# Score maxima as 768-column tiles in three banks, four views of one shared tile, and layer-1 experts by 128 places plus four experts' last 32

## The chip, the cores and the metric

One core of a Trainium2 chip runs the whole program in one launch. The metric is the device time of one execution in microseconds (us). A kernel's time here is the median of several executions; a profile is of one further execution, with a record of each instruction on each engine.

## The reference

Four sequences of 1024 tokens with 128 channels pass through two layers. Each layer has attention and then a mixture of eight experts, both with an adaptive layer norm in front and a gate behind.

```python
# layer 0: causal attention with one head, then top-2 of 8 experts, GELU, no limit on an expert's places
# layer 1, attention: 16 heads of 8 channels, not causal
scores = einsum("bhqd,bhkd->bhqk", q, k) / sqrt(8); attn = softmax(scores); ctx = attn @ v
# ... plus a second attention (rank 64) that keeps the largest 204 of 1024 weights of each row,
# both mixed by sigmoid(lam), then a norm, a feed-forward (128 -> 512 -> 128, ReLU) and a norm
# layer 1, experts: top-2 of 8, each expert takes at most int(1024 / 8 * 1.25) = 160 places per sequence
h = relu(buf @ W1[e] + b1[e]); y = h @ W2[e] + b2[e]        # buf: (expert, sequence, 160, 128)
```

Everything is float32. A softmax may subtract any number from its row that keeps the exponentials in range; the kernel subtracts the row's maximum.

## The kernel before

The program is written with pools of tiles, and its instructions are issued in the order in which Python runs (`manual_schedule`). The tile layer adds the semaphore waits. Work that may run beside the main loop is written as generators. `Part` wraps one, and a small planner (`spend`, `grouped`, `outlook`, `worth`) keeps a clock for each engine and decides after every half step which Part's next piece is put there. That sets the order on all engines.

PSUM has eight banks of 512 f32 columns. Before, they are shared out as two tiles of two banks (`psb`, tag "big"), three tiles of one bank (`ps`, tag "ms", the shared banks) and one bank (`psa`) for attention outputs.

The main loop is layer 1's 16-head attention. A unit is one sequence, one group of four heads and one half of the queries (512): 32 units. It has two interleaved streams.

- *Maxima* (`maxima`, L1622 and L1626) of the unit ahead. For 128 queries and 512 keys, two heads at a time, `pm` gets two matmuls with 32 contraction rows each, on two row groups of TensorE. VectorE reduces the 1024 columns to two maxima. 16 such tiles make a unit. `shifted` turns the maxima into an extra row of the queries (`qa`), so that scores come out already shifted.
- *Weighed scores* (`weighed`, L1638 and L1642). For 128 keys and 512 queries, one matmul `pw` per head into a shared bank, and ScalarE's exponential into `prT`. `values` (L1660) then multiplies by V into `pav`.

A half step of the loop is two `weighed` (two heads), one step of `maxima` on the two other row groups, and four `values` matmuls of the step before. There are 512 half steps; 20 steps of the maxima come earlier, in `prologue`.

Beside the loop run: `begin` (norm and projections of the next sequence), `looked` (the rank-64 attention with a search for its 204 largest weights: `pk` L1393, its maximum L1398, its exponential L1401, transposes `ptk` L1420, output `po` L1425), `end` (output projection, feed-forward `ph` L1726 and `pf` L1739) and `sends` (routing, and scattering of tokens to the experts' places in DRAM). All but `pk` take shared banks; `pk` takes a "big" tile.

After the loop comes layer 1's expert stage, `worked_on(1, ...)`. Each expert's 160 places of a sequence are loaded as two tiles of 80, transposed (L829), modulated (L886), multiplied up (`ph` L839 into a "big" tile, ReLU L844), down (`py` L854, 80 rows each), given the bias (L859), and each tile's rows are scattered to the tokens' rows by GpSimd (L864). `taken_in` adds the two results of a token. Layer 0's experts use the same function with tiles of 128 places.

Of the kernel before, what the change touches and what calls it, by code (L numbers as in the profile page):

```python
# [9 lines left out]
F32 = mybir.dt.float32  # L10
# [17 lines left out]
RUNS = (((0, 3), (3, 2)), ((0, 2),))  # L28
DEEP = (P, CAP // 2)
# [12 lines left out]
GROUPS, SOON, EARLY_P, EARLY, AHEAD = 3, 0.5, -0.3, -0.1, 0.03  # L42
LOST, LATE = 0.2, 0.5
TAX_A, TAX_D = (0.4, 3), (1.5, 2)
LAST = (18, 20, 30, -3, 33, 7, 60, 38, 50, 54)
ROWS = ["out_b", "vp_b", "ff2_b", "ln1_g", "ln1_b", "ln2_g", "ln2_b"]


@with_exitstack
def kernel(ctx: ExitStack, tc: tile.TileContext, a: dict, out: bass.AP):  # L50
# [10 lines left out]
    psb = order.enter_context(tc.tile_pool(name="big", bufs=2, space=PSUM))  # L61
    ps = order.enter_context(tc.tile_pool(name="ps", bufs=3, space=PSUM))
    psa = order.enter_context(tc.tile_pool(name="av", bufs=1, space=PSUM))

# [29 lines left out]
    row = {n: rows[:, k, :] for k, n in enumerate(ROWS)}  # L94
    router = [load(f"router{l}", [P, E], a[f"router{l}"]) for l in range(2)]
# [79 lines left out]
    o_b = load("o_b", [P, C], a["o_w"][DH : DH + 1, 0, :].to_broadcast([P, C]))  # L175
# [50 lines left out]
    def more_constants():  # L226

        nc.vector.tensor_reduce(
# [4 lines left out]
        nc.vector.tensor_scalar_mul(o_b, o_b, sig)  # L233
# [96 lines left out]
    wide = [0.0, 0.0]  # L330
    costs = {}
# [21 lines left out]
    def grouped(free=free, banks=banks, wide=wide):  # L353

        free["P"] = max(free["P"], banks[1], wide[0]) + 1.05
        del wide[0]
        wide.append(spend(("D", 1.22), free=free))
        for _ in range(2):
            del banks[0]
            banks.append(spend(("A", 0.6), free=free))  # L360

    def outlook(ops=(), ready=0.0):

        f, b, w = dict(free), list(banks), list(wide)
        spend(*ops, after=ready, shared=True, free=f, banks=b)
        for _ in range(GROUPS):
            grouped(f, b, w)
            f["P"] += 0.55
        return f["P"]
# [4 lines left out]
    class Part:  # L374
# [37 lines left out]
        def go(self):  # L412
# [11 lines left out]
            costs[self.pieces.__name__, self.done] = ops  # L424
            self.ready = spend(*ops, after=self.ready, shared=True)
            if "!" in self.wants:
                self.ready = 0.0
# [97 lines left out]
    def routed(l, b, hT, wgt, wgtT, pool, ps, places=None, hs=(0, 1)):  # L525
# [18 lines left out]
        yield "D", ("P", 0.21 * n)  # L544
# [9 lines left out]
        yield "D", ("D", 1.0), ("A", 0.3)  # L554
# [27 lines left out]
        if l == 1 or places is not None:  # L582
# [15 lines left out]
            yield "D", ("P", 0.4)  # L598
# [5 lines left out]
        if places is not None:  # L604
# [9 lines left out]
            yield "D", ("D", 1.5)  # L614
# [193 lines left out]
    def worked_on(l, q, w1, w2, b2r, act, fp, then=None):  # L808

        n, p = PLACES[l], DEEP[l]  # L810
        units = [(e, i0, m) for e in range(E) for i0, m in RUNS[l]]
        most = max(m for _, m in RUNS[l])
        gots, hss, hids, gos = {}, {}, {}, {}

        def at(u, t):
            e, i0, m = u
            return t[l][q][e * n + i0 * p : e * n + (i0 + m) * p].rearrange("(m p) c -> p m c", p=p)

        def load(u):
            m = u[2]  # L820
            gots[u] = fp.tile([P, most, C + l], F32, tag="got", bufs=4, name=f"got{l}{q}")
            got = nc.sync.dma_start(out=gots[u][:p, :m], in_=at(u, sent))
            behind(got, sent_by[l, q], "a place that any of them may have filled")

        def shift(u):
            m = u[2]
            pt = ps.tile([P, m, p], F32, tag="ms", name=f"ptg{l}{q}")
            for i in range(m):
                nc.tensor.transpose(pt[:, i, :], gots[u][:p, i, :C], ident[:p, :p])  # L829
            hss[u] = fp.tile([P, most * p], F32, tag="hs", name=f"hs{l}{q}")  # L830
            return pt, hss[u][:, : m * p]

        def up(u, k0):
            e, _, m = u
            if k0 == 0:
                hids[u] = fp.tile([P, NK, most * p], F32, tag="hid", name=f"hid{l}{q}")
            ph = psb.tile([P, 2, 512], F32, tag="big", name=f"ph{l}{q}")
            for k in range(k0, k0 + 2):
                nc.tensor.matmul(  # L839
                    ph[:, k - k0, : m * p], lhsT=w1[:, e, k * P : (k + 1) * P],  # L840
                    rhs=hss[u][:, : m * p], start=True, stop=True,
                )
            for k in range(k0, k0 + 2):
                nc.scalar.activation(  # L844
                    hids[u][:, k, : m * p], ph[:, k - k0, : m * p], act,
                    bias=b1[l][:, e * NK + k : e * NK + k + 1],
                )

        def down(u):
            e, _, m = u  # L850
            py = ps.tile([P, m, C], F32, tag="ms", name=f"py{l}{q}")
            for i in range(m):
                for k in range(NK):
                    nc.tensor.matmul(  # L854
                        py[:p, i, :], lhsT=hids[u][:, k, i * p : (i + 1) * p],
                        rhs=w2[:, e, k, :], start=(k == 0), stop=(k == NK - 1),
                    )
            y = fp.tile([P, most, C], F32, tag="y", name=f"y{l}{q}", bufs=3)
            nc.vector.tensor_tensor(y[:p, :m], py[:p], rows_of(b2r[:, e, :], m)[:p], ALU.add)  # L859
            if l == 0:  # L860
                nc.sync.dma_start(out=at(u, done), in_=y[:p, :m])
                return
            for i in range(m):
                to = nc.gpsimd.indirect_dma_start(  # L864
                    out=done[l][q][:],
                    out_offset=bass.IndirectOffsetOnAxis(ap=gos[u][:p, i : i + 1], axis=0),
                    in_=y[:p, i, :],
                    in_offset=None,
                    bounds_check=2 * T - 1,
                    oob_is_err=False,  # L870
                )
                tc.declare_no_dep(to.ins, group=f"done{l}{q}", reason="rows differ")
                tc.add_to_no_dep_group(f"done{l}{q}", to.ins)
                done_by.setdefault(q, []).append(to.ins)
# [4 lines left out]
        for i in range(len(units) + 2):  # L879
            if i < len(units):  # L880
                u = units[i]
                if i + 2 < len(units):
                    load(units[i + 2])
                pt, hs = shift(u)
                if l:
                    nc.vector.tensor_scalar(  # L886
                        hs, pt.rearrange("c m p -> c (m p)"), cols[1][:, 4, q : q + 1],
                        cols[1][:, 3, q : q + 1], ALU.mult, ALU.add,
                    )
                    gos[u] = fp.tile([P, most], mybir.dt.int32, tag="go", bufs=4, name=f"go{q}")  # L890
                    nc.vector.tensor_copy(gos[u][:p, : u[2]], gots[u][:p, : u[2], C])
                else:
                    nc.vector.tensor_copy(hs, pt.rearrange("c m p -> c (m p)"))
                yield "A!", ("P", 0.25 * u[2]), ("D", 0.15 + u[2] * p * 0.0011)
# [1114 lines left out]
```

## Time and profile before

| | us |
|---|---|
| median of 6 runs (lowest to highest) | 2047.17 (2035.39 to 2062.0) |
| the profiled execution | 2044.29 |
| its span, first to last instruction | 2042.4 |
| TensorE matmul (PE) busy | 1811.1 (89%) |
| VectorE (DVE) busy | 1285.7 (63%) |
| ScalarE (ACT) busy | 1144.8 (56%) |
| GpSimd (POOL) busy | 494.2 (24%) |
| mean granted TensorE clock | 0.933 |

PE is matmuls, PEld weight loads, which overlap matmuls. Matmuls are pipelined and their ends are modelled, so that a busy PE need not be at its peak. An f32 matmul shows as two records, one for each pass. In a line of groups: line, engine, operation, output and inputs, shapes, count, then busy us, mean ns of one, and the engine's idle time before them with what ended it. In a line of the timeline: start us, length us, engine, line, operation; in brackets the idle time before, and who ended it. "issue" is waiting that the profile does not explain. The granted clock is TensorE's, 1.00 being full speed.

### The profile page before, as it was taken

The page shows a single profiled execution, that of the slowest core. Times are in us where ns is not written, and L with a number is a line of the kernel's source. Part 1 is how long each engine was busy: PE and PEld are TensorE (multiplying, and loading weights), DVE is VectorE, ACT ScalarE, POOL GpSimd, SP SyncE. Part 2 cuts the span into 40 slices and gives each one's busy share as a digit, 9 for nine tenths or more (in the row PEclk, how much of TensorE's full clock was granted, in tenths as well). Part 3 has the DMA queues.
Part 4 walks back from the last instruction along what each step waited for, and adds up shares of the span by engine and source line. Part 5 has one row for each costly group of instructions (what it writes and reads, how often), then busy time and mean ns, then how long its engine had stood idle before and what let it go on. Part 6 is the DMA issues. An engine that isn't in the chain of part 4 may idle for free.

```text
span 2042.4 us, 33750 instructions
## 1 busy us (share of the span) xinstructions
PE 1811.1 (89%) x12805; PEld 928.1 (45%) x12805; DVE 1285.7 (63%) x3174; ACT 1144.8 (56%) x2317; POOL 494.2 (24%) x539
## 2 busy tenths in 40 slices
PE   6875888888899999998999999998998989997875
PEld 5654666552233434433343434334343424354875
DVE  4664413456788696577876666877666698842523
ACT  3442324225686755586864568785457876553432
POOL 1033345204111011103231111212211032321453
PEclk9997889898899999998998999999899999998987
DMA  8511223211000000000000000000000000003223
GB/s 283 163 42 39 63 66 87 65 34 29 19 1 27 6 2 7 1 6 6 22 18 3 6 1 6 6 22 19 4 5 5 5 9 10 8 1 114 68 69 85
DMA packets 82779, 73.11 MB, mean 36 GB/s; under 512 B 13327, under 2 KB 72035, under 8 KB 82608
## 3 DMA queue, kind: packets, MB, share of 16 engines
q1 hardware_dynamic: 73984, 56.93, 9.1%
q0 software_dynamic: 8192, 13.54, 2.3%
q8 instruction: 103, 1.69, 0.3%
q14 instruction: 68, 0.56, 0.1%
q10 hardware_dynamic: 432, 0.40, 0.1%
HBM read 35.79 MB, written 36.75 MB: 36 GB/s over the span
## 4 chain that ended last, share of the span: by engine, by line
PE 65%; DVE 12%; ACT 9%; issue 8%; POOL 2%; DMA 2%; another core or an unknown queue 1%; SPq 0%; POOLq 0%; ACTq 0%; DVEq 0%
PE pw L1638 26%; PE pav L1660 11%; PE py L854 4%; PE ph L839 4%; DVE mxh L1626 3%; PE po L1425 3%; PE pm L1622 2%; ACT prT L1642 2%; DVE nm L1398 2%; ACT junk L1492 2%; PE pf L1739 2%; ACT exq L1401 1%; PE ph L1726 1%; PE pk L1393 1%
## 5 line engine op out<-in xcount | busy, mean ns | idle before, releaser
L1626 DVE TENSOR_REDUCE mxh<-pm 128x2 f32<-128x1024 f32 x512 | 620.7, 1220 | 243.2 <-PE pm L1622 228.3
L1638 PE MATMUL pw<-qa,kg 32*128 32x512 f32 x2048 | 716.4, 660 | 56.7 <-ACT prT L1642 34.2
L1642 ACT ACTIVATE prT<-pw 128x512 f32<-128x512 f32 x1024 | 557.0, 596 | 339.6 <-PE pm L1622 199.7
L1622 PE MATMUL pm<-kg,qg 32*128 32x512 f32 x2048 | 602.6, 668 | 7.2 <-DMA qg<-qk 6.6
L1638 PEld LDWEIGHTS pw<-qa,kg 32*128 32x128 f32 x2048 | 220.2, 189 | 331.1 <-issue 160.2
L1660 PE MATMUL pav<-prT,v_more 128*9 128x256 f32 x3584 | 289.2, 395 | 0.0
L844 ACT ACTIVATE hid<-ph,b 128x160 f32<-128x160 f32 (+2 forms) x256 | 101.1, 457 | 230.3 <-PE ph L839 189.7
L1660 PEld LDWEIGHTS pav<-prT,v_more 128*9 128x9 f32 x3584 | 53.7, 89 | 356.7 <-issue 356.2
L1492 ACT ACTIVATE junk<-exq,now 128x1024 bf16<-128x1024 f32 x160 | 184.8, 1155 | 9.5 <-DVE now L1519 8.8
L1622 PEld LDWEIGHTS pm<-kg,qg 32*128 32x128 f32 x2048 | 162.2, 191 | 20.0 <-issue 8.9
L839 PE MATMUL ph<-hs,w 128*128 128x160 f32 (+2 forms) x512 | 138.2, 412 | 30.2 <-DVE hs L886 11.2
L1575 POOL TENSOR_TENSOR exq<-exq,lfq 128x512 f32<-128x512 f32 x64 | 80.9, 1286 | 343.8 <-DVE lfq L1573 336.2
L854 PE MATMUL py<-w,hid 128*128 128x128 f32 (+1 forms) x1152 | 146.1, 284 | 5.8 <-issue 5.1
L854 PEld LDWEIGHTS py<-w,hid 128*128 128x128 f32 (+1 forms) x1152 | 141.7, 181 | 12.9 <-issue 8.3
L839 PEld LDWEIGHTS ph<-hs,w 128*128 128x128 f32 x512 | 90.6, 210 | 60.2 <-issue 18.8
L859 DVE TENSOR_TENSOR y<-py,b2r 128x384 f32<-128x384 f32 (+1 forms) x64 | 29.1, 454 | 121.1 <-PE py L854 63.6
L917 POOL DMA_INDIRECT ys<-done,outof x64 | 64.2, 1003 | 167.9 <-DMA qg<-qk 68.9
L786 POOL DMA_INDIRECT sent<-xns,into x64 | 63.7, 995 | 91.9 <-DVE into L626 32.3
L864 POOL DMA_INDIRECT done<-y,go x64 | 59.6, 932 | 62.1 <-DVE y L859 17.0
L490 POOL TENSOR_TENSOR rs_l<-rs_l,mhalf 128x8 f32<-128x8 f32 (+1 forms) x10 | 14.0, 1401 | 246.3 <-DVE rs_l L489 246.3
L1425 PE MATMUL po<-sV,exT 128*128 128x129 f32 x512 | 67.4, 285 | 2.2 <-ACT exT L1421 1.1
L1425 PEld LDWEIGHTS po<-sV,exT 128*128 128x128 f32 x512 | 61.2, 195 | 16.5 <-ACT exT L1421 4.9
(532 smaller groups left out, 2221.2 us busy)
## 6 DMA issues: line engine op xcount, KB each, us to landing
w<-in_w_dram SPq DMA_DIRECT2D x32, 256.0 KB
sent<-zero SPq DMA_DIRECT2D x2, 2560.0 KB
done<-zero SPq DMA_DIRECT2D x4, 1024.0 KB
qk<-near SPq DMA_DIRECT2D x8, 512.0 KB
ys<-done SPq DMA_DIRECT2D x16, 256.0 KB
got<-sent SPq DMA_DIRECT2D x16, 192.0 KB
done<-y SPq DMA_DIRECT2D x16, 192.0 KB
sent<-nowhere SPq DMA_DIRECT2D x4, 645.0 KB
```

What stands on the lines that cost most here:

```text
L839: nc.tensor.matmul(ph[:, k - k0, : m * p], lhsT=w1[:, e, k * P : (k + 1) * P], rhs=hss[u][:, : m * p], start=True, stop=True,)
L844: nc.scalar.activation(hids[u][:, k, : m * p], ph[:, k - k0, : m * p], act, bias=b1[l][:, e * NK + k : e * NK + k + 1],)
L854: nc.tensor.matmul(py[:p, i, :], lhsT=hids[u][:, k, i * p : (i + 1) * p], rhs=w2[:, e, k, :], start=(k == 0), stop=(k == NK - 1),)
L917: nc.gpsimd.indirect_dma_start(out=y, out_offset=None, in_=done[0][b // 2][:], in_offset=bass.IndirectOffsetOnAxis(ap=outof[:, i, k : k + ...
L1425: nc.tensor.matmul(po, lhsT=exT[:, k, :], rhs=sVs[b % 2][:, k, :], start=(k == 0), stop=(k == NT - 1),)
L1492: nc.scalar.activation(junk, ex, AF.Sign, bias=now[:, i, 0:1], scale=-1.0, accum_out=now[:, i, 1:2],)
L1575: nc.gpsimd.tensor_tensor(ex[:, half(h)], ex[:, half(h)], lf[:, half(h)], ALU.subtract)
L1622: nc.tensor.matmul(pm[:, jj, :], lhsT=qg[js, t0 : t0 + P], rhs=kg[js, half(kh)], start=True, stop=True,)
L1626: nc.vector.tensor_reduce(mx[:, q, j0 : j0 + 2, kh], pm, AX.X, ALU.max)
L1638: nc.tensor.matmul(pw, lhsT=need(b, g, h)[1][js, k * P : (k + 1) * P], rhs=qas[b, g, h][js, :], start=True, stop=True,)
L1642: nc.scalar.activation(prs[b, g, h, k][:, j, :], pw, AF.Exp)
L1660: nc.tensor.matmul(to, lhsT=v, rhs=pr[:, j, cs], start=(k == 0), stop=((k, part) == (NT - 1, 1)),)
```

## The change

PSUM in the main loop is shared out anew. The three shared banks and the two "big" tiles are closed at its start. One tile of four banks, `ps4`, takes their place as four views that are handed out in turn (`Turns.split`), and one tile of three banks, `pm3`, holds the maxima. The score columns go to `pm3` in quarters of 256: three quarters make one reduce of 768 columns, first in `pm3`'s first half, then in its second. A matmul of 512 columns that would cross from one half to the other, or a bank's end, is split in two. `pk` takes two neighbouring views of `ps4`. After the loop `pm3` is closed, and three more shared tiles of one bank join the four views.

Layer 1's experts get a function of their own. An expert's first 128 places make one tile. The last 32 of four experts are loaded into one tile together; their down-projection writes four blocks of 32 output rows. Biases for these come in `b2l`.

Also: `o_b` is read into `rows` later and scaled in `prologue`; three yields of `routed` are merged into their successors; the planner knows the new tiles (`thirds`), the two-view request ("2") and other constants (`SOON` 0.5 to 0.3, `TAX_A` 3 to 2.25). In the loop the heads' order is exchanged between `weighed` and `maxima`.

```diff
+class Turns:
+    def __init__(self, pool, n):
+        self.turns = [pool.tile] * n
+    def tile(self, shape, dt, **kw):
+        self.turns.append(self.turns.pop(0))
+        return self.turns[-1](shape, dt, **kw)
+    def split(self, banks, n):
+        def of(i):
+            def view(shape, dt, **kw):
+                t = banks[: shape[0], i, : math.prod(shape[1:])]
+                return t if len(shape) == 2 else t.rearrange("p (a b) -> p a b", b=shape[2])
+            return view
+        self.banks, self.turns = banks, [of(i) for i in range(n)]
...
+    def two(self, skip):
+        if self.of[self.turns[0]] % 2:
+            self.turns.append(self.turns.pop(0))
+            skip()
+        i = self.of[self.turns[0]]
...
+        return self.banks[:, i : i + 2].rearrange("p a k -> p (a k)")
...
-    psb = order.enter_context(tc.tile_pool(name="big", bufs=2, space=PSUM))
-    ps = order.enter_context(tc.tile_pool(name="ps", bufs=3, space=PSUM))
     psa = order.enter_context(tc.tile_pool(name="av", bufs=1, space=PSUM))
+    ps_ctx = order.enter_context(ExitStack())
+    ps = Turns(ps_ctx.enter_context(tc.tile_pool(name="ps", bufs=3, space=PSUM)), 3)
+    psb = ps_ctx.enter_context(tc.tile_pool(name="big", bufs=2, space=PSUM))
...
             def looked_at(b, qt, ex, z):
-                pk = psb.tile([P, T], F32, tag="big", name="pk")
+                if general:
+                    pk = psb.tile([P, T], F32, tag="big", name="pk")
+                else:
+                    pk = ps.two(lambda: banks.append(banks.pop(0)))
...
             def maxima(b, g, h):
-                        for j0 in (2, 0):
-                            pm = psb.tile([P, 2, 512], F32, tag="big", name="pm")
+                        for j0 in (0, 2):
+                            if not three:
+                                pm = psb.tile([P, 2, 512], F32, tag="big", name="pm")
                             for jj in range(2):
                                 js = slice(32 * (j0 + jj), 32 * (j0 + jj) + 32)
+                                done_ = 0
+                                while done_ < 2:
+                                    m = 2 - done_
+                                    if three:
+                                        at = three_at[0] + len(quarters)
+                                        m = min(m, 3 - len(quarters), 2 - at % 2)
+                                        to = three[0][:, at : at + m].rearrange("p a k -> p (a k)")
...
+                                    nc.tensor.matmul(
+                                        to, lhsT=qg[js, t0 : t0 + P],
+                                        rhs=kg[js, k0 : k0 + 256 * m], start=True, stop=True,
+                                    )
...
+                                    if len(quarters) == 3 or (last_one and jj == 1 and done_ == 2 and quarters):
+                                        at, m = three_at[0], len(quarters)
+                                        nc.vector.tensor_reduce(
+                                            mx[:, quarters[0] : quarters[0] + m],
+                                            three[0][:, at : at + m], AX.X, ALU.max,
+                                        )
+                                        quarters.clear()
+                                        three_at[0] = 3 - at
...
+                    ps_ctx.close()
+                    pool = order.enter_context(tc.tile_pool(name="shared", bufs=1, space=PSUM))
+                    ps.split(pool.tile([P, 4, 512], F32, name="ps4"), 4)
+                    pool = ps_ctx.enter_context(tc.tile_pool(name="three", bufs=1, space=PSUM))
+                    three.append(pool.tile([P, 6, 256], F32, name="pm3"))
...
-                        weighed(b, g, h, k, j0)
-                        weighed(b, g, h, k, j0 + 1)
+                        weighed(b, g, h, k, 2 - j0)
+                        weighed(b, g, h, k, 3 - j0)
...
+                    ps_ctx.close()
+                    pool = order.enter_context(tc.tile_pool(name="rest", bufs=3, space=PSUM))
+                    ps.turns.extend([pool.tile] * 3)
...
+    def worked_on_own(b, w1, w2, b2r, b2l, fp, then):
...
+            if u[0] == "last":
+                parts = [
+                    (g[left * j : left * (j + 1), :], (4 * u[1] + j) * CAP + P, left)
+                    for j in range(4)
+                ]
+            else:
+                parts = [(g, u[1] * CAP, P)]
...
+                py = ps.tile([P, C], F32, tag="ms", name=f"py1{b}")
+                for k in range(NK):
+                    nc.tensor.matmul(
+                        py, lhsT=hids[e][:, k, :P], rhs=w2[:, e, k, :],
+                        start=(k == 0), stop=(k == NK - 1),
+                    )
+                out_of(("own", e), py, b2r[:, e, :])
+                if e % 4 == 3:
+                    py = ps.tile([P, C], F32, tag="ms", name=f"pz1{b}")
+                    for k in range(NK):
+                        for j in range(4):
+                            nc.tensor.matmul(
+                                py[left * j : left * (j + 1), :],
+                                lhsT=hids[e - 3 + j][:, k, P:], rhs=w2[:, e - 3 + j, k, :],
+                                start=(k == 0), stop=(k == NK - 1),
+                            )
+                    out_of(("last", e // 4), py, b2l[:, e // 4, :])
...
-    o_b = load("o_b", [P, C], a["o_w"][DH : DH + 1, 0, :].to_broadcast([P, C]))
+    o_b = row["out_b"]
```

The order in which the changed program's instructions stand, with their waits, can be listed without running it. A stretch of PE's list in the loop (semaphores are named by the engine that raises them):

```
L1800 Matmult ps4<-qa,kg1 128x512 [waits Activation] x2
L1772 Matmult pm3<-kg1,qg1 128x256
L1772 Matmult pm3<-kg1,qg1 128x256 [waits DVE]
L1772 Matmult pm3<-kg1,qg1 128x512
L1822 Matmult pav<-prT,v_more1 9x256 x4
L1800 Matmult ps4<-qa,kg1 128x512 [waits Activation] x2
L1772 Matmult pm3<-kg1,qg1 128x512 [waits DVE]
L1772 Matmult pm3<-kg1,qg1 128x256
L1772 Matmult pm3<-kg1,qg1 128x256 [waits DVE]
L1822 Matmult pav<-prT,v_more1 9x256 x4
```

L1800 is `pw`, L1772 `pm`, L1822 `pav` in the changed kernel's numbering. Each wait names a count, and so an instruction: that of a `pw` is the exponential which reads the `ps4` view written just before, that of a `pm` is the reduce of the other half of `pm3`.

## The prediction

> **What bounds the kernel now.** I read the page first, then two windows that cut the span at the first weighted score tile (458.2 us) and at the last `pav` (1861.3 us), then the waits and the timeline of the loop between them.
>
> ```profile
> span 2042.4 us, 33750 instructions
> 458.20:1861.30 1403.10, 1321.17 (x9872) 535.31 (x9872) 1004.21 (x2131) 923.30 (x1774) 293.73 (x288) 0.96 0.04 13
> 1861.30:2042.40 181.10, 127.34 (x918) 120.94 (x918) 67.48 (x248) 60.90 (x185) 71.24 (x78) 0.83 0.24 66
> ```
>
> Columns of a window: length, then busy us of PE, PEld, DVE, ACT, POOL, the granted clock, the DMA share. The loop is 1403 of 2042 us and PE is at work in 94% of it: PE sets its pace.
>
> ```profile
> L1638 PE MATMUL pw<-qa,kg 32*128 32x512 f32 x2048 | 716.4, 660 | 56.7 <-ACT prT L1642 34.2 <-DVE ro L1431 4.9 <-issue 4.8
> L1626 DVE TENSOR_REDUCE mxh<-pm 128x2 f32<-128x1024 f32 x492 | 596.8, 1220 | 221.1 <-PE pm L1622 206.3 <-remote 7.0 <-issue 2.0
> PEld pw L1638 <- ACT prT L1642: 123.3, 172, 2.9
> ```
>
> The reduces are 492, so 492 half steps (two `pw`, two `pm`, four `pav`) carry maxima; 20 more do not. The third line is what the change aims at: with three shared banks the second `pw` of a half step waits for an exponential.
>
> ```profile
> 1160.97 1.09 ACT L1642 ACTIVATE prT<-pw 128x512 f32<-128x512 f32 x2 [1.49 <-PE pm L1622]
> 1161.62 1.18 PE L1638 MATMUL pw<-qa,kg 32*128 32x512 f32 x2
> 1162.78 1.08 ACT L1642 ACTIVATE prT<-pw 128x512 f32<-128x512 f32 x2 [0.24 <-PE pw L1638]
> 1163.72 0.70 PE L1638 MATMUL pw<-qa,kg 32*128 32x512 f32 x2
> 1163.74 0.70 PE L1622 MATMUL pm<-kg,qg 32*128 32x512 f32 x2
> 1164.80 0.62 PE L1660 MATMUL pav<-prT,v_more 128*9 128x256 f32 x8
> 1164.98 1.23 DVE L1626 TENSOR_REDUCE mxh<-pm 128x2 f32<-128x1024 f32 x1 [0.43 <-PE pm L1622]
> 1165.34 0.37 PEld L1638 LDWEIGHTS pw<-qa,kg 32*128 32x128 f32 x3 [0.43 <-issue]
> ```
>
> This is one undisturbed half step: two `pw` and two `pm` on four different row groups start together at 1163.72 and take 1.08 us in all, `pav` 0.54, sum 1.62. Alone, a `pw` takes the same 1.08. From its end to its exponential are 0.08 us (1161.62 + 1.08 to 1162.78); from the start of an exponential to the matmul that it releases 0.65 (1160.97 to 1161.62). So a matmul that must wait for the exponential of the one before it pays 0.73 us beyond its 1.08. For DVE: 0.16 from the end of `pm` to the reduce (1164.82 to 1164.98).
>
> ```profile
> 205.71 0.50 PEld L839 LDWEIGHTS ph<-hs,w 128*128 128x128 f32 x2 [0.62 <-DVE hs L893]
> 206.52 0.34 PEld L839 LDWEIGHTS ph<-hs,w 128*128 128x128 f32 x1 [0.30 <-issue]
> 207.16 0.34 PEld L839 LDWEIGHTS ph<-hs,w 128*128 128x128 f32 x1 [0.30 <-issue]
> 207.80 0.34 PEld L839 LDWEIGHTS ph<-hs,w 128*128 128x128 f32 x1 [0.30 <-issue]
> 208.68 1.05 ACT L844 ACTIVATE hid<-ph,b 128x384 f32<-128x384 f32 x2 [15.46 <-PE ph L839]
> ```
>
> Here the decisive point shows. `ph` is one tile of two banks; an f32 matmul is two passes, so the loads near 206.5 belong to its first matmul and those at 207.16 and 207.80 to the second. The first activation reads only the first bank, ready near 207.4, yet starts at 208.68, after the second matmul. Dependencies are kept **by tile**, not by bank or address.
>
> **The change, part by part.** (1) Shared banks. The change makes three rotating tiles into four views of one tile `ps4`. The list of the built program's waits says what that does: of 1024 `pw` matmuls 1019 wait for the reader of the `ps4` view written just before (a `pw` in bank 2 for the exponential of bank 1). A fourth bank was meant; one is left. So the two `pw` of a half step go one after the other: 1.08 + 0.73 = 1.81 us from first to second. Behind the waiting `pw`, in order on PE, stand both `pm` and four `pav`, and for these wait DVE, and ACT's next step.
>
> (2) Maxima. `pm` becomes one tile of six 256-column quarters; A is its first three, B the others. In the list every first write to A waits for the reduce of the B just finished, and the reverse: no double buffering is left. A 768-column reduce is not in the trace; between the 1024-column row (1.22) and DVE's 128-column PSUM row (L1433, 0.35) a straight line gives 0.97, bounds 0.92 (1.22 x 3/4) and 1.22. With 0.16 before and 0.05 after it, a leg is 1.18 us. Counting from the second `pw`: half A (512, 256, leg, 256) 1.08 + 1.18 + 0.54 + `pav` 0.54 = 3.34; half B (512, leg, 512) 3.88; half C (256, leg, then 256 beside 512) 3.34. With 1.81 each: 5.15, 5.69, 5.15, mean 5.33 us, of which PE work is 3.42 and waits 1.91. DVE reduces 656 tiles of 0.97 = 636 us for 597, in the shade of these waits. A unit's 32 `pm` matmuls become 43; the columns are the same, and the extra weight loads (0.19 us each, L1622) lie under the legs. Without that cover they would cost at most 31 x 11 x 0.19 = 65 us.
>
> 492 x 5.33 = 2622; 20 half steps without maxima at 2 x 1.81 = 72; the first `pav` of 32 units, 0.46 longer, 15.
>
> (3) Side work. In the loop the other matmuls take 341 us, start to next start (po 60, ptk 44, pk 36, ph 29, pf 26, the rest small). In the list they too wait by turns: 297 tiles and 32 `pk`. An evacuation of about 0.6 (exT 0.58, qa 0.69, cn and rden 0.55) with its 0.13 to 0.2 of handing over is 0.75: 223 us. `pk` holds the tile for its maximum (1.22), scaling and exponential (1.11), 2.75 with handing over: 88 us. Before, these lay beside other tiles. Sum 341 + 311 = 652.
>
> Loop at full clock: 2622 + 72 + 15 + 652 = 3361 us, of which PE work is 1683 + 43 + 15 + 341 = 2082 and waits 1279.
>
> (4) Clock.
>
> ```profile
> 538.10:541.50 3.40, 2.23 (x16) 0.46 (x15) 1.41 (x3) 3.37 (x8) 1.99 (x2) 0.99 0.10 30
> 541.50:544.90 3.40, 3.40 (x24) 0.91 (x16) 2.16 (x7) 2.00 (x6) 0.00 (x0) 0.50 0.09 28
> 544.90:548.30 3.40, 3.40 (x36) 1.04 (x32) 3.22 (x9) 2.32 (x5) 0.00 (x0) 1.00 0.19 60
> ```
>
> After 3.4 us with PE 66% busy the next 3.4 run at clock 0.50; after a full one it is 1.00 again. The new half step has PE at work 3.42 of 5.33 us, 64%, much of it on one row group of four, so I expect half clock wherever it runs undisturbed. The 274 side blocks, about one per 20 us of such a loop, refill a window and buy some 3.4 us at full clock each: mean 0.5 x 0.83 + 0.17, about 0.6. PE work stretches by 1/0.6: 2082 / 0.6 + 1279 = 4749. Bounds: clock 1.0 gives 3361, clock 0.5 5443.
>
> The page "TensorE: Matmul & The Clock Gate" of the Trainium skill (Part 1, the clock gate) has the clock fall after an idle window of about 3.4 us. No gap here is that long, so by the rule the total would be that of full clock, about 4030; the row above had no such gap either and still fell to 0.50, so the row decides.
>
> (5) Layer-1 experts (32 experts' turns). Down-projection: eight matmuls of 0.22 us an expert, 56 us, become four an expert and sixteen 32-column ones per four experts; those run four abreast as `pav` does (eight passes in 0.62): 28 + 7, so -21. Transposes 64 to 40: -4. Scatters on POOL 64 to 40 at 0.93 + 0.3: -29, half of it on the tail's chain. SP issues 32 more loads (`last` in four pieces) and eight for `b2l`; they go out two experts ahead, beside matmuls, and cost nothing unless a batch starts late: then its first transpose waits for five landings in place of one, perhaps 4 x 0.5 us of issue a batch, 8 in all. Against it: seven shared tiles rotate there, four of them views of `ps4`; 92 such tiles, three of four waiting 0.75: +52, and a clock already at 0.83. Together +30 to +80; I take +50. `o_b` read and scaled at another place, merged yields and planner constants change order alone; PE and DVE stand idle in the waits above far longer than such a step (at most 1.4 us) could delay, and were that cover gone, ten such steps would cost 14 us.
>
> Sum: the profiled execution took 2044.3 us; less the loop's 1403.1 that is 641. 641 + 4749 + 50 = **5440 us**. The profiled run is 0.1% under the median shown, 2047.2 (2035 to 2062), so no shift is made. Likeliest range 4900 to 6200.
>
> The page "PSUM — Partial Sum Buffer" (bank collisions) asks that engines be kept apart by bank and quadrant, not by address. A and B share a bank, so even a program that waits by bank would hold B's first quarter until A is reduced; I reckon some 2500 us in all by that rule. The listed waits are wider, so this is no end of my range.
>
> **The rivals.** *Serial, but full clock*: 641 + 3361 + 30 = 4030. For it: no gap over 2 us; against it the 0.50 rows. Chance 0.22. *Serial, half clock throughout*: 641 + 5443 + 80 = 6160. For it: 1097.7 to 1101.1 us stays at 0.50 with PE never idle. Chance 0.15. *The change does what it says*, waits falling by address: the 123 us of `pw` waiting go to about 50 (DVE's slack per half step shrinks from 0.85 us to about 0.3), the experts give 25: about 1950, faster. It decides if a `pw` starts beside its neighbour before that one's exponential; the waits listed and `ph` speak against it. Chance 0.04.
>
> **How the numbers follow.** Forecast 0.57, rivals 0.22, 0.15, 0.04, waits by bank 0.02. The range takes the full-clock and half-clock ends: 4000 to 6250. Faster by over 1% (about what a measurement of this kernel tells from no change) 0.04, within 1% 0.01, slower 0.95.
>
> **Right or wrong.** Right: a `pw` starts 0.73 us or more after the one before it has ended; a half step takes 5 to 9 us; `pm` waits on `mxh`; the loop's clock is 0.5 to 0.75. Wrong: two `pw` still start together, or the loop's clock stays near 0.96 (then 4030), or the reduces lag far behind (DVE is the bound).

## The result, and the profile after

The changed kernel takes 5858.0 us (median; 5847.9 to 5863.1), the kernel before 2048.1: a ratio of 2.859 (95% interval 2.854 to 2.864). Forecast were 5440 us, range 4000 to 6250. The profiled execution took 5863.5 us.

The page's span, then two windows cut as before (length, busy us of PE, PEld, DVE, ACT, POOL, granted clock, DMA share and GB/s): the loop from its first weighted score tile to the last `pav`, and what follows it.

```profile
span 5861.7 us, 35313 instructions
448.60:5630.40 5181.80, 3951.08 (x10548) 1195.80 (x10548) 1050.58 (x2346) 1002.17 (x1774) 288.04 (x288) 0.52 0.01 4
5630.40:5861.70 231.30, 138.54 (x894) 117.12 (x894) 67.89 (x272) 62.29 (x185) 51.44 (x53) 0.74 0.18 51
```

The loop grew from 1403 to 5182 us. PE stands idle for 1231 us of it (82 before), and its clock fell from 0.96 to 0.52. The group of the reduces, and the waits of PE's weight loads (us in total, times, longest):

```profile
L1780 DVE TENSOR_REDUCE mxh<-pm 128x3 f32<-128x768 f32 x676 | 631.5, 934 | 3293.8 <-PE ps L1800 1884.0
PEld pm L1772 <- DVE mxh L1780: 1293.0, 489, 3.4
PEld ps L1800 <- ACT prT L1804: 1147.2, 522, 2.9
```

`ps L1800` is `pw`, now a view of `ps4`. Its wait for the exponential was 123 us and is 1147; the maxima's wait for their reduce was 6 and is 1293. The reduces themselves take 632 us for 597. One undisturbed half step in the timeline, and ahead of it the last reduce and the wait behind it of the half step before:

```profile
5000.06 0.96 DVE L1780 TENSOR_REDUCE mxh<-pm 128x3 f32<-128x768 f32 x1 [3.79 <-PE pm L1772]
...
5001.07 2.07 PE L1772 MATMUL pm<-kg,qg 32*128 32x512 f32 x2 [1.05 <-DVE mxh L1780]
...
5004.05 2.07 PE L1800 MATMUL ps<-qa,kg 32*128 32x512 f32 x2
5006.15 0.60 ACT L1804 ACTIVATE prT<-ps 128x512 f32<-128x512 f32 x1 [4.45 <-PE ps L1800]
...
5006.80 1.21 PE L1800 MATMUL ps<-qa,kg 32*128 32x512 f32 x1 [0.69 <-ACT prT L1804]
...
5008.95 0.96 DVE L1780 TENSOR_REDUCE mxh<-pm 128x3 f32<-128x768 f32 x1 [7.17 <-PE ps L1800]
...
5009.96 2.08 PE L1772 MATMUL pm<-kg,qg 32*128 32x256 f32 x4 [1.09 <-DVE mxh L1780]
...
5011.97 1.04 PE L1822 MATMUL pav<-prT,v_more 128*9 128x256 f32 x8
...
5012.94 2.07 PE L1800 MATMUL ps<-qa,kg 32*128 32x512 f32 x2
```

The first `pw` takes 2.07 us (1.08 at full clock). The second goes into another bank and still starts only 0.65 us after the exponential of the first has begun. The next `pm` waits for the reduce (5009.96). So does the one at 5001.07, although it goes into another bank: by the program a group of three quarters that starts with a matmul of 512 columns lies in `pm3`'s first half and starts in its first bank, and the reduce of 5000.06 reads the second half, in the other two banks. From `pw` to `pw` it is 8.90 us, where the kernel before needed 1.62; over the 512 half steps of the loop 8.90 is also the median.

For what follows, the loop of a trace is split in three: *idle* is its length less PE's busy time; *work* is PE's busy time in each stretch of granted clock, times that clock; *clock* is the rest, by which the slow clock stretches the work. Before: 1262 + 82 + 60 us (work, idle, clock). After: 2021 + 1231 + 1930.

### The profile page after: what moved, and what is told of

Its sections match the earlier page's. It is cut to its first block, busy times and chain, and to the rows that moved or that the text cites. A ratio compares the mean times of both kernels' runs of the same rounds, so it can differ in the third digit from the quotient of the medians.

```text
span 5861.7 us, 35313 instructions
## 1 busy us (share of the span) xinstructions
PE 4450.9 (76%) x13457; PEld 1587.7 (27%) x13457; DVE 1328.1 (23%) x3414; ACT 1226.4 (21%) x2317; POOL 468.8 (8%) x515
## 5 line engine op out<-in xcount | busy, mean ns | idle before, releaser
L1800 PE MATMUL ps<-qa,kg 32*128 32x512 f32 x2048 | 2085.5, 1118 | 560.1 <-ACT prT L1804 353.1
L1772 PE MATMUL pm<-kg,qg 32*128 32x512 f32 (+1 forms) x2724 | 1756.6, 905 | 540.7 <-DVE mxh L1780 535.6
L1780 DVE TENSOR_REDUCE mxh<-pm 128x3 f32<-128x768 f32 x676 | 631.5, 934 | 3293.8 <-PE ps L1800 1884.0
L1804 ACT ACTIVATE prT<-ps 128x512 f32<-128x512 f32 x1024 | 611.3, 597 | 3176.3 <-PE ps L1800 2880.6
L1800 PEld LDWEIGHTS ps<-qa,kg 32*128 32x128 f32 x2048 | 500.9, 302 | 1736.8 <-ACT prT L1804 1147.2
L1772 PEld LDWEIGHTS pm<-kg,qg 32*128 32x128 f32 x2724 | 496.3, 302 | 1309.8 <-DVE mxh L1780 1293.0
L1822 PE MATMUL pav<-prT,v_more 128*9 128x256 f32 x3584 | 466.8, 614 | 0.0
L1822 PEld LDWEIGHTS pav<-prT,v_more 128*9 128x9 f32 x3584 | 57.5, 95 | 541.7 <-issue 541.5
L923 PE MATMUL ph<-hs,w 128*128 128x384 f32 (+2 forms) x376 | 114.4, 448 | 9.7 <-DVE mxh L1787 4.2
L1552 PE MATMUL ps<-sV,exT 128*128 128x129 f32 x512 | 116.8, 418 | 3.1 <-DVE r_lg L663 2.3
L1552 PEld LDWEIGHTS ps<-sV,exT 128*128 128x128 f32 x512 | 108.4, 322 | 28.4 <-issue 22.8
```

Source lines behind the costliest of these rows:

```text
L923: nc.tensor.matmul(ph[:, k - k0, :n], lhsT=w1[:, e, k * P : (k + 1) * P], rhs=hs, start=True, stop=True)
L1552: nc.tensor.matmul(po, lhsT=exT[:, k, :], rhs=sVs[b % 2][:, k, :], start=(k == 0), stop=(k == NT - 1),)
L1772: nc.tensor.matmul(to, lhsT=qg[js, t0 : t0 + P], rhs=kg[js, k0 : k0 + 256 * m], start=True, stop=True,)
L1780: nc.vector.tensor_reduce(mx[:, quarters[0] : quarters[0] + m], three[0][:, at : at + m], AX.X, ALU.max,)
L1800: nc.tensor.matmul(pw, lhsT=need(b, g, h)[1][js, k * P : (k + 1) * P], rhs=qas[b, g, h][js, :], start=True, stop=True,)
L1804: nc.scalar.activation(prs[b, g, h, k][:, j, :], pw, AF.Exp)
```

## Experiments

The runs below were made on other chips than the first profile, on which the kernel before takes 1970 us in place of 2047; each is set against that. The runs with one of the two tiles apart, with filling and with bursts are one execution each; windows and waits are always those of one profile.

### One of the two joined tiles at a time

Theory: both joined tiles make waits by tile, and the clock falls with them. Rivals: one of the two is the whole loss, or the extra work is.

```diff
 # shared banks apart (pk becomes two such tiles, with a maximum and an exponential for each half)
-ps.split(pool.tile([P, 4, 512], F32, name="ps4"), 4)
+pool = order.enter_context(tc.tile_pool(name="shared", bufs=4, space=PSUM)); ps.turns = [pool.tile] * 4
 # maxima apart: one matmul of 512 columns and one reduce each
-three.append(pool.tile([P, 6, 256], F32, name="pm3"))
+three.append(ps_ctx.enter_context(tc.tile_pool(name="three", bufs=3, space=PSUM)))
...
+p1 = three[0].tile([P, 512], F32, tag="pm1", name="pm1")
```

> The changed kernel with the four shared banks as four tiles of one bank each (pk becomes two of them, with a maximum and an exponential for each half); the maxima stay one tile of six quarters. Theory (the loss comes from waits by tile, one from each of the two joined tiles): the two pw of a half step start together again, and only the maxima wait, one leg of 1.18 us a half step. PE work per half step is then near 2.2 us and the waits near 1.25; with 341 us of side matmuls that is a loop of about 2100 us at full clock and some 3300 us at a clock of 0.55, so a total of 2800 to 4000 us, and waits of pw for prT below 150 us. Rival (the shared banks are not what serialises; the maxima's half-bank tiles are the whole loss): within 10% of the changed kernel's 5858 us. Rival (the maxima cost nothing, the shared tile is the whole loss): near 2100 us.

> The changed kernel with the maxima in three tiles of one bank, each with one matmul of 512 columns and one reduce of 512 (984 in the loop, about 0.65 us each, 640 us in all for 636); the shared banks stay one tile with four views. Theory: no leg is left for the maxima, the pw stay serial: a half step is 1.81 + 1.08 (second pw beside both pm) + 0.54 = 3.43 us at full clock, of which 0.73 is wait. Loop 2430 us at full clock, about 3780 us at a clock of 0.55; total 3100 to 4460 us, the low clock the likelier. Rival (the maxima are the whole loss): near 2100 us. Rival (the shared banks are the whole loss): within 10% of 5858 us.

> Both of the above at once: four shared tiles of one bank, three maxima tiles of one bank, all else as in the changed kernel. Theory: no wait of the joined tiles is left, the clock comes back to about 0.95 and the loop to 1350 to 1450 us; total 1960 to 2070 us, near the kernel before. If the fourth shared bank takes away most of the 123 us for which PE waited for exponentials, it is under 2000 us. Rival (the extra work of the change, its matmuls, loads or order, carries a good part of the loss): over 2300 us.

The main wait that is left with the shared banks apart, with the maxima apart, and three with both apart, each from the waits of that kernel:

```profile
PEld pm L1787 <- DVE mxh L1795: 1296.1, 493, 4.9
```

```profile
PEld ps L1812 <- ACT prT L1816: 1408.2, 825, 2.9
```

```profile
PEld pav L1849 <- ACT prT L1831: 94.7, 124, 1.5
PEld pm L1777 <- DVE mxh L1781: 80.3, 119, 3.8
PEld pw L1827 <- ACT prT L1831: 59.2, 111, 0.9
```

| | total | loop | work | idle | clock | granted clock | after the loop |
|---|---|---|---|---|---|---|---|
| changed (first chip) | 5858 | 5182 | 2021 | 1231 | 1930 | 0.52 | 231 |
| shared banks apart | 3787 | 3228 | 1520 | 618 | 1090 | 0.59 | 144 |
| maxima apart | 4404 | 3766 | 1625 | 713 | 1428 | 0.55 | 224 |
| both apart | 1976 | 1422 | 1287 | 62 | 73 | 0.95 | 143 |

Each separation takes away its own wait and leaves the other's (with the shared banks apart no `pw` waits for its exponential any more, with the maxima apart no `pm` in the loop for its reduce); both together bring the kernel back to a ratio of 1.002 (0.999 to 1.004). So nearly the whole loss lies in the two joined tiles, and the new experts and the new order carry none of it that is seen here. Waits alone are a third: of the 3760 us between the first and the last row 1169 are idle time, 734 are work that lies one after another instead of abreast on four row groups, and 1857 are clock. The single gains (1954 and 1416; the 2% by which the loop differs from chip to chip is small beside them) add up to less than 3760, since the clock only comes back when both are gone (its term falls by 840 and 502 one at a time, by 1857 together). Both single runs came out at the low-clock end of what was expected.

### What holds the clock down

PE idles in 24% of the changed loop, in gaps of 3.2 us at most. Are the gaps the cause, or how little of the array works? Filling matmuls, whose result nobody reads, are put into the waits, with 128 rows or with 32. Their result takes a bank of its own, so that in this run and the three others with filling or bursts `ps4` has three views in place of four.

```diff
+def fill(n):    # 128 rows; the second kernel takes [:32] of both operands
+    nc.tensor.matmul(filled[0][:, :n], lhsT=ident, rhs=rows.rearrange("p k c -> p (k c)")[:, C : C + n], start=True, stop=True)
...
 weighed(b, g, h, k, 2 - j0)
+fill(256)
 weighed(b, g, h, k, 3 - j0)
...
+if not quarters and (jj or done_):     # a group of maxima that waits inside a half step
+    fill(512)
```

> The changed kernel plus filling work: in each half step one matmul of 128 rows and 256 columns between the two pw, and one of 128 rows and 512 columns ahead of each group of maxima that has to wait inside a half step (its result goes to a bank of its own and is not read; the shared tile has three views in place of four, which by the theory is the same). That adds about 1.6 us of PE work at full clock to each half step, within its 1.9 us of waits. Theory (the clock falls because too little of the PE array is at work, and rises when it is filled): clock in the loop 0.85 or more, loop 3400 to 3900 us in place of 5182, total 4000 to 4500 us: more work and less time. Rival (the clock is set by something else, the number of waits or the chip): clock still near 0.52, and the filling work, twice as long at that clock, no longer fits the waits: over 6200 us.

> The same filling matmuls with 32 rows in place of 128: PE is as seldom idle as with 128, but a quarter of the array's rows works. Theory (the share of the array at work counts, not the share of time in which PE is busy): the clock stays at 0.6 or below and the total is over 5800 us. Rival (the gaps count): the clock rises as with 128 rows, total 4000 to 4500 us.

With 128 rows: 6359 us, loop 5737 us at clock 0.52, although PE was now busy for 5398 of it. With 32 rows: 5776 us, loop 5162 us at 0.52. The theory, as I had put it, fell: filling did not raise the clock, and the first run has the clock and the total that its rival had named. (The second has the clock of its theory; its total is just under the 5800 us.) Neither do gaps explain it: PE is idle in only 6% of the first of these loops. Three consecutive windows of that loop show why:

```profile
1448.50:1451.90 3.40, 3.40 (x14) 0.73 (x13) 0.96 (x1) 0.00 (x0) 0.00 (x0) 0.50 0.00 0
1451.90:1455.30 3.40, 3.40 (x16) 3.40 (x16) 0.00 (x0) 0.00 (x0) 0.00 (x0) 0.50 0.00 0
1455.30:1458.70 3.40, 1.40 (x10) 0.85 (x9) 2.98 (x6) 0.59 (x1) 0.00 (x0) 1.00 0.00 0
```

PE is busy throughout in the first and in the second. After the first the clock stays at 0.50; after the second, sixteen matmul passes on all 128 rows (`po`), it is 1.00. In all these traces the clock changes only on a grid of 3.41 us. So I worked out for each window of this grid what share of the array's rows was at work: each matmul's streaming time (512 columns take 0.54 us at full clock) times its rows over 128, with the four column groups of `pav` counted once, against what the array could take at full speed. In nine profiles (of the kernel before, twice, the changed one, and the runs with shared banks apart, maxima apart, both apart, old banks and filling), over 8383 windows of the loops, the next window is at full clock where this share is over 0.46 and at half clock otherwise, with 62 exceptions. (By where in its record a matmul's streaming time is put, this count comes to some 40 to 110, and the later counts move in the same measure.) Busy time alone does not do it: in the twelve profiles with which the bound was compared in the end, PE is busy without a pause in 5191 windows, and after 3250 of these the clock is half. The bound is the same from either clock. At half clock the share cannot pass 0.50, so a loop that has fallen only comes back after a window in which nearly the whole array is full all the time. The filled half step has a share of about 0.59 at full clock and half of it at half clock: it could hold either state, and sat in the lower.

This can be tested: the same filling, plus a short burst that reaches 0.50.

```diff
+if n % 4 == 0 and j0 == 0:     # once in eight half steps
+    for _ in range(4):
+        fill(512)
```

> The changed kernel with the filling work of 128 rows in each half step (as in the run of 6359 us) and, once in eight half steps, four filling matmuls of 128 rows and 512 columns one after the other: 8.3 us at half clock, 4.3 us at full. Theory, read from 8383 windows of 3.41 us in the runs so far: a window runs at full clock where, in the one before it, the rows at work, as a share of what the array can take at full speed, were over 0.46, and this bound is the same at half clock, where the share can't pass 0.50. With the filling a half step has a share of about 0.59 at full clock and 0.28 at half: it holds either state. The bursts (share 0.50 over a whole window at half clock) bring it to full clock, and there it stays until side work with a low share: clock in the loop over 0.8, loop 3700 to 4200 us, total 4300 to 4850 us. Rival (the filling does not hold the clock; after a burst one window is full and the next is half again): clock below 0.6, total over 6500 us.

> The changed kernel with the bursts alone, without the filling between them. Theory: a half step of the changed kernel has a share of about 0.30 at full clock, under the bound, so after each burst the clock falls again within a window or two: clock in the loop under 0.6, total 5700 to 6200 us. Rival (a burst is enough by itself): clock over 0.8, total under 4700 us.

With filling and bursts: 5664 us, loop 5051 us at clock 0.67. Bursts alone: 5930 us, loop 5310 us at 0.56. The second is as its theory had it; the first fits neither its theory nor its rival. Windows of the first, and its whole loop:

```profile
1415.70:1419.10 3.40, 3.40 (x14) 0.81 (x11) 2.06 (x2) 0.00 (x0) 0.00 (x0) 0.50 0.00 0
1419.10:1422.50 3.40, 3.40 (x6) 1.33 (x5) 0.09 (x1) 0.00 (x0) 0.00 (x0) 0.50 0.00 0
1422.50:1425.90 3.40, 3.34 (x11) 1.19 (x12) 0.00 (x0) 0.60 (x1) 0.00 (x0) 1.00 0.00 0
...
1449.80:1453.20 3.40, 2.55 (x16) 0.89 (x15) 0.69 (x1) 0.00 (x0) 0.00 (x0) 1.00 0.01 2
1453.20:1456.60 3.40, 3.40 (x8) 1.11 (x7) 0.00 (x0) 0.60 (x2) 0.00 (x0) 0.50 0.00 0
```

```profile
416.00:5466.60 5050.60, 4699.47 (x13061) 1543.04 (x13060) 1050.77 (x2346) 1001.76 (x1773) 285.70 (x287) 0.67 0.01 4
```

A burst lies in the second window; from 1422.50 the clock is full, and the filling holds it for nine windows, until the wait for a side tile (`qa`) leaves one thin (2.55 us busy). Full stretches have a median of 13.7 us with filling and bursts, 6.8 us with bursts alone, 3.4 us in the changed kernel. Adding 64 bursts made the filled kernel 695 us shorter: here more work was less time. But I expected 4300 to 4850 us: I had not reckoned how often side work ends a full stretch, after which the loop waits at half clock for the next burst (half-clock stretches last 34 us in the median). Bound and trap stand; that such filling could carry the loop is not shown. In the three profiles taken after the bound was fixed (these two and one below) it was wrong in 23 of 3441 windows.

### The rest of the change

> The kernel before, unchanged, profiled on the chip of the runs beside it, so that stages can be set side by side. The earlier runs on another chip than that of the first profile were some 4% shorter with this kernel (1970 us); theory: the stage before the loop is what is shorter, about 412 us, and the loop between 1365 and 1403 us. Rival: all stages are shorter in proportion (441, 1350, 174 us).

The kernel before, on these chips: 427.5 us ahead of the loop, 1378.3 in it, 170.2 after it; on the first chip 458.2, 1403 and 181. The stages shrink by 7%, 2% and 6%: neither expectation fits exactly, and why chips differ is open. This profiled execution (1977.9 us) is 7 us longer than the median, so gains by stage against it are that much too large in sum.

```diff
 # old banks in the loop: the new split of PSUM left out, pk in a "big" tile again
-ps.split(pool.tile([P, 4, 512], F32, name="ps4"), 4)
-three.append(pool.tile([P, 6, 256], F32, name="pm3"))
...
-pool = order.enter_context(tc.tile_pool(name="rest", bufs=3, space=PSUM))
+pool = order.enter_context(tc.tile_pool(name="rest", bufs=7, space=PSUM))     # after the loop
 # old experts as well (second kernel), and the pools after the loop as before
-worked_on_own(b, w1, w2, b2r, b2l, fp, lambda b=b: next_one(b))
+worked_on_old(1, b, w1, w2, b2r, AF.Relu, fp, lambda b=b: next_one(b))
 # old constants (third kernel: the first one, with these)
-GROUPS, SOON, EARLY_P, EARLY, AHEAD = 3, 0.3, -0.3, -0.1, 0.03
+GROUPS, SOON, EARLY_P, EARLY, AHEAD = 3, 0.5, -0.3, -0.1, 0.03
-TAX_A, TAX_D = (0.4, 2.25), (1.5, 2)
+TAX_A, TAX_D = (0.4, 3), (1.5, 2)
```

> All of the change but the new banks of the loop: three shared tiles and two of two banks for the maxima as in the kernel before, and the layer-1 experts, constants and order as in the changed kernel; after the loop seven shared tiles of one bank. Theory: the loop is again 1403 us within 1%, its clock 0.96; the stage after it shrinks by 15 to 40 us from 181 (down-projections -21, transposes -4, scatters -15): total 2005 to 2035 us, a ratio of 0.98 to 0.995. Rival (the experts' many small matmuls or the lowered clock there cost more than they save): over 2060 us.

> The banks of the kernel before (as in the run with a ratio of 0.975) and also its layer-1 experts and its pools after the loop; of the change there remain the constants of the planner, the order of the row groups, the extra maximum in the shift, the place of o_b's load and the merged steps. Theory (the gain of that run is the experts'): the stage after the loop is back at about 175 us, total 1950 to 1970 us, ratio 0.99 to 1.0. Rival (the gain is the planner's constants and the order): ratio 0.975 to 0.98 again, with the loop under 1370 us.

> The kernel with a ratio of 0.975 (all of the change but its banks in the loop) with the planner's two changed constants put back (how late a piece may be ready, and how much work of ACT may lie ahead). Theory (the gain outside the layer-1 experts, 1.0% in the run with the old experts, is in the stage before the loop and in the order of the row groups): ratio 0.97 to 0.98, loop within 8 us of 1365 us. Rival (the constants made the loop 13 us shorter): loop 1375 to 1385 us, ratio 0.98 to 0.99.

| | ratio to before (95%) | ahead of the loop | loop | after it |
|---|---|---|---|---|
| kernel before | 1 | 427.5 | 1378.3 | 170.2 |
| old banks | 0.975 (0.969 to 0.980) | 411.3 | 1365.1 | 142.3 |
| ... and old experts | 0.990 (0.987 to 0.994) | 409.0 | 1365.3 | 170.6 |
| old banks, old constants | 0.987 (0.981 to 0.992) | 413.3 | 1375.6 | 143.6 |

The loop and the stage after it, with old banks:

```profile
411.30:1776.40 1365.10, 1298.86 (x9872) 526.39 (x9872) 1017.76 (x2162) 920.73 (x1774) 285.84 (x283) 0.97 0.05 13
1776.40:1918.70 142.30, 99.02 (x897) 90.93 (x894) 66.10 (x272) 59.86 (x185) 55.65 (x58) 0.85 0.31 86
```

Without its new banks the change is a gain of 2.5%, more than the 0.98 to 0.995 expected, and the fastest version of all runs: 28 us from the new experts, 13 from the loop, some 16 ahead of it. With the old experts the ratio is that of the theory, but the loop under 1370 us is the rival's: the experts are the larger part of the gain and not all of it. The constants carry most of the loop's 13 as far as one profile each can tell (my theory said they did not; the rival's 1375 to 1385 us and its ratio came true). Which edit shortens the first stage was not taken apart.

### Is the fourth shared bank worth a maxima bank?

With both kinds of tiles apart the loop is 1422 us, 57 more than with the old banks. This run keeps three shared banks and gives the maxima four tiles of one bank.

```diff
-three.append(ps_ctx.enter_context(tc.tile_pool(name="three", bufs=3, space=PSUM)))
+three.append(ps_ctx.enter_context(tc.tile_pool(name="three", bufs=4, space=PSUM)))
-tc.tile_pool(name="shared", bufs=4, space=PSUM)
+tc.tile_pool(name="shared", bufs=3, space=PSUM)
```

> The kernel with a ratio of 0.975 (three shared banks, all of the change but its banks), with the maxima's four banks as four tiles of one bank in place of two of two: 984 reduces of 512 columns at 0.64 us in place of 492 at 1.22 (DVE +35 us), pk in two of them with two maxima and two exponentials. It tells apart what the run with four shared banks and three maxima tiles lost in its loop (57 us): theory (the bank taken from the maxima): the loop stays within 15 us of 1365 us and pm waits for reduces stay under 30 us, ratio 0.97 to 0.985. Rival (the halved reduces and the split pk): the loop is near 1422 us, ratio about 1.0.

Loop 1396.2 us, ratio 0.990 (0.983 to 0.997); PE waits for reduces almost nowhere (1.5 us of its matmuls'). So 31 of the 57 us come with the halved reduces and the split `pk`, 26 with the bank that moved. Theory and rival each had about half. The split into 31 and 26 is rough: executions of one of these kernels differ by up to 13 us, and `pk` moved with the bank, from the shared tiles to the maxima's. In the same lists of waits the weight loads of `pw` stand 59 us for exponentials with four shared banks (118 with the old banks), but those of `pm` 80 us for reduces (8), and those of `pav`, next to nothing with the old banks, 95 us for exponentials: the fourth bank halves the wait at which the change aims and makes others as large next to it.

## Why the prediction was right, and where it was off

- *Waits by tile: right.* Read from `ph` in the trace before and from the program's waits. Matmuls into four different banks waited for each other's readers because the banks were one tile. (The loads quoted from `ph` run one pass ahead of the matmuls: 206.52 is the load of the second matmul's first pass. But a pass of the matmuls starts at each of these times, and the first matmul has ended by 207.4, so the reading stands.) The page "Perfetto Trace Analysis" of the Trainium skill (Matmuls) has independent matmul groups rotate through different banks so that evacuation lies beside the next group; the changed kernel does so by address and got no such cover (1147 us of waiting for exponentials), until the banks were tiles of their own.
- *The legs: right within 8%.* From a `pw`'s end to the next one 0.73 us were forecast, 0.69 measured (in brackets at 5006.80, and the median of the 512 half steps), a little under the 0.73 that was to be the sign of being right; the maxima's leg 1.18 forecast, 1.09 measured (at 5009.96), with a reduce of 0.93 for 0.97. At full clock, in the kernel with bursts, half steps last 5.2 to 5.6 us (for example 1429.01 to 1434.63), for a forecast mean of 5.33; filling in the waits does not lengthen them much.
- *PE's work 2082 and waits 1279: right within 4%.* Measured 2021 and 1231.
- *The clock of about 0.6: the term that was mis-sized.* It is 0.52. PE's busy time became 3951 us instead of 2082/0.6 = 3470: +481. Waits -48 and the stage ahead of the loop -10 leave +423, the whole gap from 5440 to the profiled 5863. The step that failed is that 274 side blocks "buy some 3.4 us at full clock each": the loop has 47 full stretches, 4% of its time. The reason given for the half clock was not the right one either: it went by PE's busy time (64% of a half step) and put no number to "much of it on one row group of four", and with PE busy for 94% of the filled loop the clock was still 0.52. A block has to fill a window almost wholly with all rows (0.46 of at most 0.50), and with the blocks' own evacuation waits few do. Weighing rows would have told it in advance: the bound of 0.46 holds for 407 of 410 windows in the trace before, and a serial half step, with 1.08 us of all-row equivalents in its `pw` and `pm` and 0.54 in `pav`, comes to 1.62 / 5.33 = 0.30.
- *The rival "half clock throughout"* (6160) had this mechanism; it was too long because work and waits were a little smaller, the few full stretches were left out, and the stages around the loop took less. Full clock (4030) and waits by address (1950) fell. The rule of the Trainium skill's page "TensorE: Matmul & The Clock Gate" (Part 1), a fall after an idle window, would have given 4030; the filled loop at 0.52 with PE busy 94% of the time contradicts idleness as the measure.
- *After the loop, +50: right as a sum, in part by luck.* It was picked from +30 to +80. 231.3 less 181.1 is 50.2. In its parts: the new experts give 28 (142.3 for 170.2; forecast was -21 - 4 - 15 + 8 = -32), the joined tile costs 80 (224 with it, 144 without, forecast 52 and something for the clock, which there is 0.74 with it and 0.85 without).
- *Constants, `o_b` and merged steps at nothing: nearly.* Together with the heads' order they are worth about 1% (20 us), more than the 14 us allowed for.

## What to carry to other kernels

Double buffering is a property of what the tile layer, which tracks the dependencies, takes for one thing: cutting one tile into views of several banks gives addresses to rotate, not waits that rotate, and it undid two buffers at once here. When a matmul that ran abreast with others becomes serial, price three things, the wait, the lost company and the clock; here the clock was the largest. And take a bundle apart before dropping it: the same change without its new banks beats both kernels by its other parts.

## What was not expected of the hardware

The granted clock behaves like a switch with a bound on the array's share at work, measured against full speed: over 0.46 of the rows in one window of 3.41 us gives full clock in the next (85 exceptions in 11824 windows of twelve profiles), whichever clock it was measured at. As half clock halves the share, slow loops stay slow: the same filled half step ran at full clock for a median of 13.7 us after a burst and otherwise at 0.50. The share is by rows: PE busy without a pause, but on 32 of 128 rows in part of the time, counts as little. Whether something in the chip counts rows, or something that goes along with them, these runs do not tell.
